# A graph-attention layer whose softmax is one-hot: the last four row blocks reordered, and the unused general path's transfers moved to another queue

## The chip, the cores and the metric

The kernel runs on one core of a Trainium2 chip. The core has five engines with instruction streams of their own: TensorE (PE in the profile; PEld is its weight load), VectorE (DVE), ScalarE (ACT), GpSimd (POOL) and SyncE (SP). Each works through its stream in order, and they meet through semaphores. 16 DMA engines move data between HBM and SBUF. Here SP issues nearly all plain transfers, and POOL the gathers, whose addresses are computed on the chip.

The metric is device time in microseconds (us), the median of several executions. The profile is one further execution, whose span runs from the first instruction to the last. Times such as "at 215.65" are counted from the start of that span.

## The reference, cut to what matters

```python
x: (4096, 512)   adj: (4096, 4096), about 0.4% of it nonzero, values up to 1e9
W: (512, 4*512)  a: (4, 2*512, 1)

ht  = (x @ W).reshape(N, 4, 512).transpose(1, 0, 2)
src = einsum('hnd,hd->hn', ht, a[:, :512, 0])
dst = einsum('hnd,hd->hn', ht, a[:, 512:, 0])
e   = leaky_relu(src[:, :, None] + dst[:, None, :], 0.01) + adj[None]
att = softmax(e, axis=-1)
g   = einsum('hij,hjd->hid', att, ht).mean(axis=0)
y   = x + g
out = (y - mean(y)) / sqrt(var(y) + 1e-5)      # over each row of 512
```

The adjacency values are so large that in nearly every row the largest one leads the next by far more than the attention terms can make up. The softmax is then 1 at that column c and 0 elsewhere, for all four heads, so g = x[c] @ (mean of W over the heads).

## The kernel before, in words

The kernel has two paths. `leading_rows` computes the whole output by the shortcut, and at the same time tests whether every row leads by enough. If a row does not, the flag `any_bad` is positive and `general` computes the exact attention. With these inputs the flag is zero, so `general` (line 529 on) is compiled and never entered. The branch is at line 62: every engine loads the flag (L61) and jumps. A hint placed in the loop tells PE, ACT, DVE and POOL about that branch; SP has no hint.

Rows are taken in 32 blocks of 128, numbered 0 to 31. For one block:

1. SP loads the block of adj, 2 MB (L118). DVE takes the maximum of each segment of 32 columns (L163) and finds the leading segment (`find_segment`, L170 and L172).
2. POOL computes its row number (L174), gathers the segment again from HBM ("lead", L176) and keeps its start (L181).
3. `find_column`: DVE finds the position inside the segment (L198), POOL adds the start (L200) and gathers the 128 rows x[c] ("y", L186).
4. `turn`: PE transposes y (L213), ACT copies the result to SBUF as `yt` (L215). `products`: PE multiplies with the mean weight, four matmuls per block that add up in PSUM ("o", L228). `residual` adds x by one more matmul with the identity (L221).
5. The row statistics are made on ACT (`stats`, L250 and L252) with a small POOL part (`rstd`, L255 to L257), or on DVE with one square root on ACT (`moments`, `factor`). The row is scaled on ACT (`finish`, L261) or on DVE (`normalise`, L297) into `hold`, the SBUF array that held x and now holds the output, and SP stores it (`store`, L313).

The order of the work is written out by hand, and each engine runs it in program order. One step t of the loop works on several blocks at once: it reduces block t, finds the column of block t-2, and turns and multiplies block t-3. The last blocks are treated in their own ways. Blocks 24 to 27 (`BEHIND` to `LATE`-1) are multiplied without x, put by in SBUF (`put_by`, L241), and get x later (`add_x`, L244, three on POOL and one on DVE). Blocks 28 and 29 get x by `residual` matmuls issued in the last step (L442, L443). Block 30 gets it on DVE from PSUM (L511). Block 31 is handled in two halves of columns, each with its own PSUM bank (L266, L270, L304, L309, L310); its column is found in the full row of adj (L206) and needs no segment.

Stores are held back: SP's queue issues its loads first, and the stores of blocks 0 to 23 follow the last loads (L465 to L468). Then come the stores of blocks 28, 29, 24 and 25, 30, 26 and 27, and 31 (L523 to L525). The semaphores of SP's transfers are eight in rotation, so a transfer is not issued before the eighth one before it has landed, and a store whose data is late holds up all later ones. The gathers on POOL have eight semaphores of their own.

Of the kernel before, what the change touches and what calls it, by code (L numbers as in the profile page):

```python
# [20 lines left out]
P = 128  # L21
# [45 lines left out]
def leading_rows(ctx, tc, x, adj, W, a, out, ident, v, n_bad, any_bad):  # L67
# [100 lines left out]
    def find_segment(ib):  # L168
        seg = seg_of.pop(ib)
        nc.vector.max(out=top[:, ib, :], in_=seg)  # L170
        at = small.tile([P, 8], U32, name="at")
        nc.vector.max_index(at, top[:, ib, :], seg)  # L172
        row = small.tile([P, 1], U32, name="row")
        nc.gpsimd.tensor_tensor(row, at[:, 0:1], first[:, ib : ib + 1], op=OP.add)  # L174
        lead = lead_pool.tile([P, E], F32, name="lead")
        nc.gpsimd.indirect_dma_start(  # L176
            out=lead, out_offset=None, in_=adj_segs,
            in_offset=bass.IndirectOffsetOnAxis(ap=row[:, :1], axis=0),
        )
        start = at_of[ib] = small.tile([P, 1], U32, name="start")  # L180
        nc.gpsimd.tensor_tensor(start, at[:, 0:1], width, op=OP.mult)  # L181
        lead_of[ib] = lead

# [78 lines left out]

    def residual_in_halves(ib):
        o_ps[ib] = [psum.tile([P, D // 2], F32, name="o") for _ in range(2)]
        for k, o in enumerate(o_ps[ib]):
            nc.tensor.matmul(o, ident, hold[:, ib, ts(k, D // 2)], start=True, stop=False)  # L266
# [22 lines left out]
    def factor(ib, shift=False):  # L289
        nc.vector.reciprocal(rt[ib], rt[ib])  # L290
        if shift:
            nc.vector.scalar_tensor_tensor(
                nm[:, ib : ib + 1], mean_var[ib][:, 0:1], -1.0, rt[ib], op0=OP.mult, op1=OP.mult
            )
# [111 lines left out]
    COLUMN, PROJECT, STATS, FINISH = 2, 3, 4, 6  # L406

    for t in range(NB):
# [92 lines left out]
    report(pg)  # L501
    turn(NB - 1)
# [14 lines left out]
    finish(BEHIND + 2)  # L517
    finish(BEHIND + 3)
# [4 lines left out]
    for ib, n in ((NB - 4, 1), (NB - 3, 1), (BEHIND, 2), (NB - 2, 1), (BEHIND + 2, 2)):  # L523
        store(nc.sync, ib, n)
# [4 lines left out]
def general(ctx, tc, x, adj, W, out, ident, v, n_bad):  # L529
# [20 lines left out]
    with ExitStack() as pre:  # L550
# [3 lines left out]
        for g in range(NCH):  # L554
            nc.gpsimd.dma_start(x_sb[:, ts(g, Q), :], x_blocks[:, ts(g, Q), :])
        for kb in range(KB):
            nc.gpsimd.dma_start(w_sb[:, kb, :], w_blocks[:, kb, :])
# [29 lines left out]
    def block(ib):  # L587
# [4 lines left out]
        nc.gpsimd.dma_start(adj_t, adj[ds(ib, P, NB), :])  # L592
# [39 lines left out]
        nc.gpsimd.dma_start(r, x[ds(ib, P, NB), :])  # L632
# [10 lines left out]
        nc.gpsimd.dma_start(out[ds(ib, P, NB), :], r)  # L643
# [35 lines left out]
```

## Time and profile before

| what | value |
|---|---|
| median of 3 runs | 235.95 us (235.95 to 236.46) |
| the profiled execution's own time | 236.21 us |
| its span | 234.6 us |
| mean granted clock of TensorE | 0.975 |
| busy: PE, DVE, ACT, POOL | 195.2, 188.4, 111.6, 101.2 us |
| moved by DMA | 97.21 MB, mean 414 GB/s |
| DMA engines busy, from 0 to 202 us / from 207.6 to 229.3 us | 1.00 / 0.97 |
| a 128x512 add on POOL (L244) / on DVE (L244) | 1.28 / 0.67 us |
| a residual matmul, 128x512 (L221) | two passes, 0.43 us each |

The profile is a page of views: the share of time each engine is busy, the span in 40 slices, the queues, the chain of work that ended last, and the groups of instructions. The chain starts at the last instruction of the program and goes back, at each step, to what released it; it ends in the work that set the end. A busy engine that is not in the chain sets nothing. Further views list a stretch in order of time, or one line's instructions with the waits on their queue (marked with a small q, as PEldq).

### The profile page before, as it was taken

To read this page: it belongs to the slowest core of one execution; us is meant where nothing else is said; L and a number is where in the kernel's file an instruction comes from. 1 tells how busy PE (TensorE), PEld (TensorE's weight loads), DVE (VectorE), ACT (ScalarE), POOL (GpSimd) and SP (SyncE) were. 2 spreads that over 40 slices of the span, in tenths; PEclk is the share of its full clock that TensorE was granted. 3 is DMA by queue.
4 is the path that set the end of the run, shared out by engine and by line. 5 is a ranking of instruction groups with operands and counts; after the bars stand their busy time and mean duration, and the time that the engine had idled before them with its cause. 6 is when DMAs were issued, how large, how long until landed. Compare 5 with 4: busy or idle time off the path is not lost.

```text
span 234.6 us, 2498 instructions
## 1 busy us (share of the span) xinstructions
PE 195.2 (83%) x683; PEld 101.4 (43%) x683; DVE 188.4 (80%) x302; ACT 111.6 (48%) x267; POOL 101.2 (43%) x215
## 2 busy tenths in 40 slices
PE   0188929999999999999979879797998968698990
PEld 0034514756565655555534333242443423244460
DVE  1736875589869995999589989998799999989672
ACT  2012011255474747474758354646464645166582
POOL 1012232414527462646353645464365464549130
PEclk9999977999999999999999999999799999999998
DMA  6999999999999999999999999999999999999985
GB/s 226 439 428 426 443 425 430 415 440 412 440 420 426 424 437 434 425 424 428 427 432 433 425 433 422 432 418 429 425 432 418 422 425 427 411 425 419 417 355 210
DMA packets 13697, 97.21 MB, mean 414 GB/s; under 512 B 2152, under 2 KB 2664, under 8 KB 7792
## 3 DMA queue, kind: packets, MB, share of 16 engines
q1 hardware_dynamic: 10080, 88.08, 88.9%
q0 software_dynamic: 3584, 8.92, 9.6%
q8 instruction: 6, 0.10, 0.2%
q14 instruction: 11, 0.09, 0.1%
q10 hardware_dynamic: 16, 0.02, 0.0%
HBM read 88.62 MB, written 8.39 MB: 414 GB/s over the span
## 4 chain that ended last, share of the span: by engine, by line
DMA 45%; POOL 17%; issue 15%; PE 10%; DVE 9%; ACT 1%; POOLq 0%; SPq 0%; DVEq 0%
DMA adj_t<-in_adj_dram 42%; DVE seg L163 8%; PE o L228 7%; POOL lead L176 6%; POOL y L186 5%; DMA y<-in_x_dram,col 3%; POOL sd L256 2%; PE o L270 2%; POOL start L181 1%; POOL row L174 1%; POOL col L200 1%; PE tp L213 1%; PE o L221 1%; ACT yt L215 1%; POOL sd L255 1%
## 5 line engine op out<-in xcount | busy, mean ns | idle before, releaser
L163 DVE TENSOR_REDUCE seg<-adj_t 128x64 f32<-128x2048 f32 (+1 forms) x68 | 146.0, 2149 | 32.7 <-DMA adj_t<-in_adj_dram 32.3
L228 PE MATMUL o<-w_sum,yt 128*128 128x512 f32 x248 | 115.1, 605 | 1.7 <-ACT yt L215 1.7
L228 PEld LDWEIGHTS o<-w_sum,yt 128*128 128x128 f32 x248 | 44.5, 191 | 54.8 <-issue 42.3
L215 ACT COPY yt<-tp 128x512 f32<-128x512 f32 x32 | 18.8, 588 | 44.3 <-PE tp L213 44.3
L176 POOL DMA_INDIRECT lead<-in_adj_dram,row x32 | 32.3, 1010 | 15.5 <-POOL row L174 15.0
L186 POOL DMA_INDIRECT y<-in_x_dram,col x32 | 30.9, 965 | 15.4 <-POOL col L200 15.2
L318 PE MATMUL o<-hold,ident 128*128 128x512 f32 x32 | 18.9, 745 | 17.5 <-DMA hold<-in_L_gnn_W_dram 17.5
L213 PE MATMUL tp<-ident,y 128*128 128x128 f32 x128 | 20.0, 280 | 12.6 <-DMA y<-in_x_dram,col 12.6
L221 PE MATMUL o<-hold,ident 128*128 128x512 f32 x52 | 27.3, 611 | 0.0
L213 PEld LDWEIGHTS tp<-ident,y 128*128 128x128 f32 x128 | 14.9, 143 | 25.4 <-issue 25.0
L174 POOL TENSOR_TENSOR row<-at,first 128x1 uint32<-128x1 uint32 x32 | 6.1, 190 | 42.0 <-DVE at L172 42.0
L336 ACT COPY wt<-tp 128x512 f32<-128x512 f32 x16 | 9.2, 587 | 31.4 <-PE tp L334 31.4
L200 POOL TENSOR_TENSOR col<-start,within 128x1 uint32<-128x1 uint32 x31 | 5.9, 190 | 40.1 <-DVE within L198 40.1
L235 ACT ACTIVATE sq<-hold 128x512 f32<-128x512 f32 x32 | 19.8, 619 | 0.0
L342 PEld LDWEIGHTS pv<-at_d,wt 128*128 128x128 f32 x128 | 16.3, 191 | 6.8 <-ACT wt L336 4.0
L318 PEld LDWEIGHTS o<-hold,ident 128*128 128x128 f32 x32 | 7.4, 243 | 26.7 <-POOL row L174 11.0
L319 ACT ACTIVATE w_sum<-o 128x512 f32<-128x512 f32 x4 | 2.4, 598 | 33.9 <-PE o L318 33.9
L261 ACT ACTIVATE hold<-o,nm,sd 128x512 f32<-128x512 f32 x24 | 17.2, 771 | 0.0
L252 ACT ACTIVATE sq<-o,nm 128x512 f32<-128x512 f32 x24 | 16.5, 688 | 0.8
L342 PE MATMUL pv<-at_d,wt 128*128 128x2 f32 x128 | 15.3, 244 | 0.6 <-ACT wt L336 0.6
L250 ACT ACTIVATE sq<-o 128x512 f32<-128x512 f32 x24 | 14.6, 609 | 0.0
L334 PEld LDWEIGHTS tp<-ident,hold 128*128 128x128 f32 x64 | 7.9, 142 | 6.9 <-issue 6.9
(85 smaller groups left out, 139.8 us busy)
## 6 DMA issues: line engine op xcount, KB each, us to landing
adj_t<-in_adj_dram SPq DMA_DIRECT2D x27, 2048.0 KB, 31.3
hold<-in_x_dram SPq DMA_DIRECT2D x7, 1024.0 KB, 33.2
adj_t<-in_adj_dram SPq DMA_DIRECT2D x6, 1024.0 KB, 25.7
out_dram<-hold SPq DMA_DIRECT2D x10, 512.0 KB, 15.2
adj_t<-in_adj_dram SPq DMA_DIRECT2D x8, 512.0 KB
hold<-in_L_gnn_W_dram SPq DMA_DIRECT2D x4, 1024.0 KB
out_dram<-hold SPq DMA_DIRECT2D x2, 1024.0 KB
hold<-in_x_dram SPq DMA_DIRECT2D x2, 512.0 KB, 14.1
```

Of the source, the lines that this page charges most:

```text
L163: nc.vector.tensor_reduce(seg_of[ib][:, ts(k, S // n)], adj_t[ib][:, ts(k, N // n)].rearrange("p (s e) -> p s e", e=E), axis=AX.X, op=OP.max,)
L176: nc.gpsimd.indirect_dma_start(out=lead, out_offset=None, in_=adj_segs, in_offset=bass.IndirectOffsetOnAxis(ap=row[:, :1], axis=0),)
L186: nc.gpsimd.indirect_dma_start(out=y, out_offset=None, in_=x, in_offset=bass.IndirectOffsetOnAxis(ap=col[:, :1], axis=0),)
L213: nc.tensor.transpose(tp[:, kb, :], y[:, ts(kb, P)], ident)
L215: nc.scalar.copy(yt, tp)
L221: nc.tensor.matmul(o_ps[ib], ident, hold[:, ib, :], start=start, stop=False)
L228: nc.tensor.matmul(o_ps[ib], yt_of[ib][:, kb, :], w_sum[:, kb, :], start=(start and kb == 0), stop=(kb == KB - 1),)
L235: nc.scalar.activation(sq, hold[:, ib, :], AF.Square, accum_out=xx[:, ib : ib + 1])
L252: nc.scalar.activation(sq, o, AF.Square, bias=nm[:, i], accum_out=sd[:, i])
L261: nc.scalar.activation(hold[:, ib, :], o_ps.pop(ib), AF.Identity, bias=nm[:, i], scale=sd[:, i])
L318: nc.tensor.matmul(o, ident, hold[:, w_at + kb * H + h, :], start=(h == 0), stop=(h == H - 1))
L342: nc.tensor.matmul(pv[:, kb, h : 2 * H : H], wt[:, k, :], at_d[:, k, h : 2 * H : H], start=(k == 0), stop=(k == KB - 1),)
```

## The change

The change has five parts.

- **General path.** All plain transfers of `general`, which POOL issued, are issued by SP. The path is still not entered.
- **Late residuals.** The two `residual` matmuls of blocks 28 and 29 are gone. A new `add_residual` adds x on DVE while reading the product from PSUM, as was already done for block 30. In return, `add_x` of block 27 goes from DVE to POOL, and block 28 is finished on ACT and no longer on DVE. Blocks 26 and 27 are finished on POOL (`finish_on_chip`) and no longer on ACT. `turn` of block 29 comes ahead of block 31's two x matmuls.
- **One-input shift.** In `factor`, one `scalar_tensor_tensor` becomes a `tensor_scalar` with the same operands.
- **Gathers.** `find_segment` is split. In the last step, the segment of block 31 is fetched by POOL after the y gather of block 30, and its start is not computed. Only `add_x` of block 24 stands between that fetch and the y gather of block 31; `add_x` of 27, 25 and 26 follow.
- **Stores.** The held stores go out in another order (`HELD`), two-block stores mixed with the two of four blocks, and the last ones are 28, 24 and 25, 26 and 27, 29, 30, 31.

```diff
     def find_segment(ib):
...
-        at = small.tile([P, 8], U32, name="at")
+        at = at_of[ib] = small.tile([P, 8], U32, name="at")
         nc.vector.max_index(at, top[:, ib, :], seg)
+        if ib < NB - 1:
+            fetch_segment(ib)
+
+    def fetch_segment(ib):
+        at = at_of.pop(ib)
         row = small.tile([P, 1], U32, name="row")
         nc.gpsimd.tensor_tensor(row, at[:, 0:1], first[:, ib : ib + 1], op=OP.add)
...
+    def finish_on_chip(ib):
+        i, h = slice(ib, ib + 1), hold[:, ib, :]
+        o_ps.pop(ib)
+        nc.gpsimd.tensor_scalar(h, h, sd[:, i], nm[:, i], op0=OP.mult, op1=OP.add)
+
+    def add_residual(ib):
+        nc.vector.tensor_add(hold[:, ib, :], o_ps[ib], hold[:, ib, :])
+        o_ps[ib] = hold[:, ib, :]
...
-            nc.vector.scalar_tensor_tensor(
-                nm[:, ib : ib + 1], mean_var[ib][:, 0:1], -1.0, rt[ib], op0=OP.mult, op1=OP.mult
+            nc.vector.tensor_scalar(
+                nm[:, ib : ib + 1], mean_var[ib][:, 0:1], rt[ib], -1.0, op0=OP.mult, op1=OP.mult
             )
...
+    HELD = ((8, 2), (10, 2), (0, Q), (12, 2), (14, 2), (Q, Q), (16, 2), (18, 2), (20, 2), (22, 2))
...
-            residual(LATE)
-            residual(LATE + 1)
...
-    for ib in range(0, 2 * Q, Q):
-        store(nc.sync, ib, Q)
-    for ib in range(2 * Q, BEHIND, 2):
-        store(nc.sync, ib, 2)
+    for ib, n in HELD:
+        store(nc.sync, ib, n)
     find_column(NB - 2)
+    fetch_segment(NB - 1)
     add_x(nc.gpsimd, BEHIND)
-    add_x(nc.gpsimd, BEHIND + 1)
     find_column_in_row(NB - 1)
-    add_x(nc.gpsimd, BEHIND + 2)
+    for ib in (LATE - 1, BEHIND + 1, BEHIND + 2):
+        add_x(nc.gpsimd, ib)
     products(LATE, KB - 1, KB)
+    turn(NB - 3)
     residual_in_halves(NB - 1)
-    turn(NB - 3)
     products(NB - 3, 0, KB - 1)
+    bound(0)
+    stats(BEHIND)
+    add_residual(LATE)
     moments(LATE)
+    bound(1)
+    factor(LATE, shift=True)
     for ib in range(BEHIND, NB):
         find_inner(ib)
-    bound(0)
     products(NB - 3, KB - 1, KB)
-    stats(BEHIND)
-    factor(LATE)
-    normalise(LATE, o_ps.pop(LATE))
-    bound(1)
     turn(NB - 2)
+    finish(LATE)
+    moments(LATE - 1)
+    stats(BEHIND + 1)
     bound(2)
-    add_x(nc.vector, LATE - 1)
-    stats(BEHIND + 1)
-    moments(LATE - 1)
-    products(NB - 2, 0, 2)
     bound(3)
     test()
+    products(NB - 2, 0, KB - 1)
     pg = count()
-    products(NB - 2, 2, KB - 1)
     stats(BEHIND + 2)
     rstd(slice(BEHIND, BEHIND + 2))
     rstd(slice(BEHIND + 2, BEHIND + 3))
+    add_residual(NB - 3)
+    turn(NB - 1)
     moments(NB - 3)
     report(pg)
-    turn(NB - 1)
     factor(LATE - 1, shift=True)
     factor(NB - 3)
     normalise(NB - 3, o_ps.pop(NB - 3))
     finish(BEHIND)
     finish(BEHIND + 1)
+    finish_on_chip(BEHIND + 2)
+    finish_on_chip(BEHIND + 3)
     products(NB - 2, KB - 1, KB)
     products_of_half(NB - 1, 0)
     products_of_half(NB - 1, 1)
-    nc.vector.tensor_add(hold[:, NB - 2, :], o_ps[NB - 2], hold[:, NB - 2, :])
-    o_ps[NB - 2] = hold[:, NB - 2, :]
+    add_residual(NB - 2)
     moments(NB - 2)
     stats_of_half(NB - 1, 0)
     factor(NB - 2)
     normalise(NB - 2, o_ps.pop(NB - 2))
-    finish(BEHIND + 2)
-    finish(BEHIND + 3)
...
-    for ib, n in ((NB - 4, 1), (NB - 3, 1), (BEHIND, 2), (NB - 2, 1), (BEHIND + 2, 2)):
+    for ib, n in ((LATE, 1), (BEHIND, 2), (BEHIND + 2, 2), (NB - 3, 1), (NB - 2, 1)):
         store(nc.sync, ib, n)
...
-            nc.gpsimd.dma_start(x_sb[:, ts(g, Q), :], x_blocks[:, ts(g, Q), :])
+            nc.sync.dma_start(x_sb[:, ts(g, Q), :], x_blocks[:, ts(g, Q), :])
...
-        nc.gpsimd.dma_start(adj_t, adj[ds(ib, P, NB), :])
+        nc.sync.dma_start(adj_t, adj[ds(ib, P, NB), :])
...
```

The other three transfers of `general` (the weights, x of a block and the store) change in the same way.

More of the change, by code (lines that the diff above doesn't have):

```diff
@@ L179, in find_segment @@
         )
-        start = at_of[ib] = small.tile([P, 1], U32, name="start")
-        nc.gpsimd.tensor_tensor(start, at[:, 0:1], width, op=OP.mult)
         lead_of[ib] = lead
+        if ib < NB - 1:
+            start = at_of[ib] = small.tile([P, 1], U32, name="start")
+            nc.gpsimd.tensor_tensor(start, at[:, 0:1], width, op=OP.mult)
     def gather_rows(ib, col):
@@ L554, in general @@
         for g in range(NCH):
-            nc.gpsimd.dma_start(x_sb[:, ts(g, Q), :], x_blocks[:, ts(g, Q), :])
+            nc.sync.dma_start(x_sb[:, ts(g, Q), :], x_blocks[:, ts(g, Q), :])
         for kb in range(KB):
-            nc.gpsimd.dma_start(w_sb[:, kb, :], w_blocks[:, kb, :])
+            nc.sync.dma_start(w_sb[:, kb, :], w_blocks[:, kb, :])
         for g in range(NCH):
@@ L631, in block @@
         r = turned.tile([P, D], F32, name="y_g")
-        nc.gpsimd.dma_start(r, x[ds(ib, P, NB), :])
+        nc.sync.dma_start(r, x[ds(ib, P, NB), :])
         nc.vector.tensor_add(r, r, held)
@@ L642, in block @@
         nc.vector.tensor_scalar(r, r, mv[:, 0:1], sd, op0=OP.subtract, op1=OP.mult)
-        nc.gpsimd.dma_start(out[ds(ib, P, NB), :], r)
+        nc.sync.dma_start(out[ds(ib, P, NB), :], r)
     with tc.For_i(0, NB, 1) as ib:
```

## The prediction, on record before the run

> **What bounds the kernel now.** I read the page first: the 40 slices, then the chain that ended last.
>
> ```profile
> DMA  6999999999999999999999999999999999999985
> ...
> DMA 45%; POOL 17%; issue 15%; PE 10%; DVE 9%; ACT 1%; POOLq 0%; SPq 0%; DVEq 0%
> ```
>
> The DMA engines are full up to slice 38, so until about 223 us bytes set the pace, and no part of the change removes a byte. Only the tail can be shortened. The chain in order of time shows it:
>
> ```profile
> 196.17 7.27 DMA y<-in_x_dram,col
> ...
> 204.21 3.57 PE o L228 x8
> 207.78 1.72 PE o L221 x4
> ...
> 224.40 0.44 PE tp L213 x4
> 224.83 0.86 PE o L228 x2
> 225.69 3.55 PE o L270 x16
> 229.27 0.44 DVE halves_st L304
> ...
> 230.69 0.56 ACT hold L310
> ```
>
> From 203.6 to 229.3 PE works nearly without a gap; then the last block's statistics, its scaling, its store at 231.29 (SP's stream) and 2.3 us to landing. The two residual matmuls are in this chain: 1.72 us. What could stop PE from starting sooner are the y gathers. TensorE's queue reads ahead, so the time at which it passes the wait for a gather is the time at which the gather landed. L213's view in four narrow windows gives 207.6, 213.0, 218.5 and 222.8 for blocks 28 to 31; the second and fourth:
>
> ```profile
> L213 PEldq EVENT_SEMAPHORE  x1: 51/51/51, 213.0 to 213.0; - x1
> ...
> L213 PEldq EVENT_SEMAPHORE  x1: 51/51/51, 222.8 to 222.8; - x1
> ```
>
> PE transposed these blocks at 209.33, 215.01, 219.93 and 224.23: slacks of 1.8, 2.0, 1.4 and 1.5 us. So 1.72 us less on PE brings two gathers to the edge. POOL's timeline says when they are issued:
>
> ```profile
> 211.54 0.19 POOL L200 TENSOR_TENSOR col<-start,within 128x1 uint32<-128x1 uint32 x1
> 212.00 0.97 POOL L186 DMA_INDIRECT y<-in_x_dram,col  x1 [0.27 <-POOL col L200]
> 212.99 2.50 POOL L244 TENSOR_TENSOR hold<-hold,adj_t 128x512 f32<-128x512 f32 x2
> 215.65 0.96 POOL L186 DMA_INDIRECT y<-in_x_dram,col  x1 [0.16 <-PE tp L213]
> ```
>
> Last, both ends of the program, from the views of L665 (the entry) and L674 (the exit):
>
> ```profile
> L665 POOLq MOVE  x4: 29/29/35, 0.2 to 0.4; - x4
> ```
>
> ```profile
> L674 SPq EVENT_SEMAPHORE  x14: 17/28/28, 232.8 to 234.5; - x14
> ```
>
> SP's twelve closing waits run from 232.84 to 233.62, some 0.063 apart; the last one is for the last store, and 0.94 us of barrier follows.
>
> **What the Trainium skill says.** "DMA: Bandwidth & Descriptors", section "SWDGE vs HWDGE vs iDMA": POOL's gathers and SP's transfers feed different queues in each DMA engine, which takes them in turn. The trace agrees: a store of 512 KB took 15.2 us to land behind others, while these four y gathers took 6.05, 6.97, 6.48 and 7.12 us from POOL's issue to PE. So the new order of stores should hardly move the gathers, though they scatter by 0.5 us either way. "Runtime: NRT & Kernel Launch", section "Instruction fetch mechanics": a taken branch whose target is outside the fetched pages stalls. In the trace SP's branch costs nothing visible (0.05 us, next wait 0.18 us later).
>
> **The change part by part**, in the clock of the profile before.
>
> *Start.* In the built program the four register moves that POOL made for its transfers before the first barrier (0.21 to 0.42, 0.06 apart) are SP's now. POOL reaches the barrier last, SP idles there. All starts 0.24 us sooner: -0.24 (bounds -0.3 and 0).
>
> *PE up to block 30.* Turning 28 follows at 207.61 where the residuals stood (its gather: 207.55): -1.72. Five matmuls later PE is free at 214.14 - 1.72 = 212.42, but block 29's gather, which is not moved, lands at 213.02: PE idles 0.6 us. That gap costs little: the two x matmuls of block 31 (0.86 us) now stand behind the turn and cover ACT's copy, which before left PE idle (1.27 us from turn to product). Products of 29 start at 213.13 + 0.44 + 0.86 = 214.43, before at 216.28: -1.85. Turning 30 then falls at 219.93 - 1.85 = 218.08. Its gather: `within` ends at 210.34, POOL answers 0.09 later, 0.70 from the add to the gather as at 209.71, so 211.13 and not 212.00; landing 218.48 - 0.87 = 217.6. It is in time.
>
> *Block 31's gather.* POOL: gather of 30 until 212.10, row 0.2, lead from 212.82 to 213.79, one add of 1.28 to 215.1, then 0.16: issued at 215.26 (DVE's index is ready at 214.84), before 215.65. Landing 222.77 - 0.39 = 222.38. PE would be free at 222.10 (219.36 for the products of 30, three of 0.86, the count 0.15). So the gather decides: turn 31 at 222.48, before 224.23: -1.75. Everything PE does after it keeps that; its end is 227.52.
>
> *DVE.* It gains two adds from PSUM (0.69 as at L511), loses one `add_x` (0.67) and one scaling from PSUM (0.81); scaling 29 from SBUF takes 0.55 as for block 30. In order: after L206 (214.84) `xm`, add 28, its moments to 216.6, `xg` at 217.42 (after PE), two small ones, eight maxima of 0.09. The last needs block 31's lead, issued 2.4 us later than before: landing 215.75 + 2.42 = 218.2, needed at 218.6. Moments of 27 to 219.7, the test to 220.9 (before 222.3), add and moments of 29 to 222.4, report to 222.8, scaling of 29 at 224.1 (it waits for ACT's root behind `yt` of 31), add of 30 at 224.65, and by the distances before (2.89) scaling of 30 ends near 227.4. PE ends at 227.52: hidden, by 0.1 us only.
>
> *ACT.* `yt` of 30 at 218.72, finish 28 (0.8), root, stats of 25 and 26 (1.5 each) to 223.1; `yt` of 31 wanted at 223.12. Hidden, again with nothing over.
>
> *POOL and SP.* rstd of 26 ends at 224.3, then two `tensor_scalar` of 512 elements, which no row shows: below, 0.19 us (a small one, L255); above, the two-input add, 1.28. "GPSIMD Engine Reference", sections 3.1 and 4.1: one-input operations are roughly line-rate, about 1 cycle per element for up to two operations, 1.8 for a plain loop. At its 1.2 GHz that is an estimate of 0.45 to 0.77 us, plus 0.19: I take 0.8, range 0.19 to 1.28. Store of 26 and 27 at 226.0, ahead of 29, 30 and 31 on SP. The held stores drain until about 226; 1.5 MB (24 to 27, 29, 30) at 410 GB/s end near 230, when store 31, issued at 231.29 - 1.75 = 229.54, begins to move. Hidden up to 1.3 us per operation.
>
> *One-input shift.* 0.16 us either way: 0 (bounds ±0.05).
>
> *End.* This one costs. `general` now uses SP's semaphores, so in the built program the untaken side has SP wait for all eight of them and raise them. The eighth wait is for store 31. Only after it come the twelve closing waits, which before ran while the store was landing: 233.62 - 232.84 = 0.78. The eight new waits themselves hide: before, SP stood at its closing waits 1.55 us after it issued store 31, eight more at 0.063 make 2.05, and the landing takes 2.3. All other engines then wait for SP at the barrier. +0.78; bounds 0.5 (closing waits already met might pass faster) and 1.0 (one more jump).
>
> Sum: -0.24 - 1.75 + 0.78 = -1.21. Against the profiled execution: 236.21 - 1.21 = 235.0. That execution lies 0.26 above the median, so 235.95 - 1.21 = **234.75 us**.
>
> **Rivals.**
>
> *Gathers take the place of the residuals.* PE then only waits longer. For it: all four slacks are 1.4 to 2.0 us, and the gathers scatter. Against: two gathers are issued sooner. If block 31's takes 7.5 to 7.8 us and lands at 222.8 to 223.1, the tail gains 1.35 to 1.05: 235.15 to 235.45. A shorter one gains nothing more, since ACT and DVE have nothing over.
>
> *No gain: the stores set the end.* The DMA engines stay full to 226 whatever PE does. If the drain is 1 us longer or the mixed packets slower, store 31 queues, and about 235.9 results. Against: 0.74 busy after 226.
>
> *SP's branch.* SP's skipped code grows from 45 to 82 instructions in the built program. If the target is then no longer fetched, a stall stands before the closing waits. No view shows what one costs; 0.3 us of it is hidden, 0.8 would take the gain below 0.7, and 1.5 would end at 235.95. Against: before, the jump was free.
>
> *Slower: POOL's scaling holds up SP.* If one `tensor_scalar` takes T, store 26-27 goes out at 224.4 + 2T; it and three more stores need about 4.6 us to land (1.28 MB at 410 GB/s, 1.5 of latency). Later than now, 233.6 - 0.54, from T = 2.0; at T = 2.5 the landing is at 234.0 and the time 235.95 + 0.4 + 0.54 = 236.9. For it: two operations in one instruction are unknown here. Against: an add with two inputs takes 1.28.
>
> **How the numbers follow.** The forecast 0.56 (234.3 to 235.15), gathers 0.17, stores 0.09, SP's branch 0.08, POOL 0.10. A measurement of this kernel tells about 0.3% from no change, 0.7 us: faster means below 235.24. Forecast and part of the gathers: 0.62. Same: rest of the gathers, stores, branch: 0.28. Slower: POOL, 0.10. The range 234.2 to 236.0 leaves POOL and some edges out.
>
> **What would show it.** Right: no L221 after 207 us; PE idle near 213 for 0.6 us before block 29's turn; block 31's turn near 222.2 (0.24 sooner in all); SP's closing waits all behind the last landing. Wrong: POOL's two operations above 1.3 us, a DVE wait for lead near 218, PE waiting past 222.8 for block 31, or a pause of SP after its branch.

## The result, and the profile after

The changed kernel takes 236.91 us (median of 16 executions, 236.24 to 238.29) against 236.23 us for the kernel before (16 executions, 235.63 to 237.01): a ratio of 1.0038, with a 95% interval of 1.0024 to 1.0052. It is slower by 0.7 us. The forecast was 234.75 us. Executions in a slower state (two in e1, one in e10, two in e12, one in e17) are left out of all medians and ratios below.

The profiled execution took 236.44 us, with the same span as before, 234.6 us. The page looks much the same too: the DMA engines are full for as many slices, and the chain that ended last has less PE (8% and not 10%) and more POOL and issue.

```profile
DMA  6999999999999999999999999999999999999985
...
DMA 36%; issue 23%; POOL 23%; PE 8%; DVE 6%; ACT 1%; SPq 1%; POOLq 0%; DVEq 0%
```

The chain in order of time (start, length, what) answers to the one shown of before:

```profile
201.43 7.39 DMA y<-in_x_dram,col
208.96 0.63 PE tp L219 x4
209.59 4.38 PE o L234 x10
...
224.44 3.58 PE o L285 x16
228.04 0.44 DVE halves_st L319
...
229.53 0.56 ACT hold L325
```

The two residual matmuls are gone, and TensorE ends at 228.00, 1.23 us sooner than the 229.23 of before. The forecast was 1.71 in the clock of before, so 1.95 with the 0.24 us by which everything was to start sooner. The first row shows where it was lost: block 28's gather, issued at 201.43 (before: 201.50), took 7.4 us and not 6.05. TensorE now waits for it, where before it had 1.8 us in hand. This is L219 (the transposes) in the window from 208 to 210:

```profile
L219 PEldq EVENT_SEMAPHORE  x1: 51/51/51, 208.9 to 208.9; - x1
...
  DMA y<-in_x_dram,col: 2.5, 1
```

Blocks 28 to 31 are transposed at 208.96, 213.80, 218.72 and 222.92 (before: 209.33, 215.01, 219.93, 224.23). The gather of block 31 was passed at 222.31, so it was not what held its turn.

POOL's timeline shows the moved gathers, nearly where they were foreseen. Block 31's was to be issued at 215.26 and went out at 215.93, though the start was 0.24 us sooner:

```profile
211.54 0.97 POOL L192 DMA_INDIRECT y<-in_x_dram,col  x1 [0.60 <-POOL col L206]
...
213.00 0.97 POOL L181 DMA_INDIRECT lead<-in_adj_dram,row  x1 [0.27 <-issue]
213.99 1.28 POOL L250 TENSOR_TENSOR hold<-hold,adj_t 128x512 f32<-128x512 f32 x1
215.93 0.97 POOL L192 DMA_INDIRECT y<-in_x_dram,col  x1 [0.66 <-issue]
```

The last stores are L328 on SP's queue. The row gives the shortest, median and longest issue in ns, and below it the time from issue to landing:

```profile
L328 SPq DMA_DIRECT2D out_dram<-hold x5: 332/383/1044, 225.9 to 230.1; - x5
...
DMA to landing us min/median/max: 2.8/2.8/2.8
```

The same view of the kernel before:

```profile
L313 SPq DMA_DIRECT2D out_dram<-hold x5: 332/332/333, 225.5 to 231.3; - x5
...
DMA to landing us min/median/max: 2.3/2.3/2.3
```

Block 31's store goes out at 230.12, 1.17 us sooner than before, but lands 2.8 us later and not 2.3. One issue, that of blocks 26 and 27, took 1.04 us. Then the exit (L62 is the untaken branch's join, L686 the closing waits):

```profile
L62 SPq EVENT_SEMAPHORE  x9: 17/17/17, 231.9 to 232.9; - x9
```

```profile
L686 SPq EVENT_SEMAPHORE  x14: 17/28/28, 232.9 to 234.5; - x14
```

Of the nine waits at L62 the last is for the last landing: SP passes it at 232.88. Then come the twelve closing waits, up to 233.62. In the kernel before, SP passed the same landing at 233.62 as its last closing wait. So in this pair of profiles the landing is 0.74 us sooner, and the closing waits behind it take 0.74 us: the barrier begins at the same time. (0.24 of these 0.74 us is the earlier start of the program.)

A second profile of the unchanged changed kernel (e12 below) took 236.88 us and had a span of 235.0 us. It has block 28 late again (transposed at 209.19), TensorE's end at 228.37, an issue of 1.08 us, and a landing 2.85 us after the issue at 230.48.

### The profile page after: what moved, and what is told of

It is laid out like the page before. It is cut to its first block, busy times and chain, and to the rows that moved or that the text cites. A ratio compares the mean times of both kernels' runs of the same rounds, so it can differ in the third digit from the quotient of the medians.

```text
span 234.6 us, 2493 instructions
## 1 busy us (share of the span) xinstructions
PE 193.9 (83%) x679; PEld 100.5 (43%) x679; DVE 188.0 (80%) x303; ACT 111.1 (47%) x266; POOL 103.9 (44%) x217
## 4 chain that ended last, share of the span: by engine, by line
DMA 36%; issue 23%; POOL 23%; PE 8%; DVE 6%; ACT 1%; SPq 1%; POOLq 0%; DVEq 0%
DMA adj_t<-in_adj_dram 30%; POOL lead L181 8%; POOL y L192 7%; PE o L234 5%; DVE seg L163 5%; DMA y<-in_x_dram,col 3%; DMA lead<-in_adj_dram,row 3%; POOL sd L262 3%; POOL row L179 2%; POOL start L188 2%; PE o L285 2%; POOL col L206 1%; PE tp L219 1%; POOL sd L261 1%; SPq L118 1%
## 5 line engine op out<-in xcount | busy, mean ns | idle before, releaser
L234 PEld LDWEIGHTS o<-w_sum,yt 128*128 128x128 f32 x248 | 45.3, 194 | 55.8 <-issue 43.9
L333 PE MATMUL o<-hold,ident 128*128 128x512 f32 x32 | 17.9, 710 | 17.5 <-DMA hold<-in_L_gnn_W_dram 17.5
L219 PE MATMUL tp<-ident,y 128*128 128x128 f32 x128 | 19.7, 277 | 12.6 <-DMA y<-in_x_dram,col 12.5
L227 PE MATMUL o<-hold,ident 128*128 128x512 f32 x48 | 26.2, 629 | 0.0
L219 PEld LDWEIGHTS tp<-ident,y 128*128 128x128 f32 x128 | 14.5, 141 | 25.3 <-issue 24.3
L333 PEld LDWEIGHTS o<-hold,ident 128*128 128x128 f32 x32 | 6.9, 226 | 26.2 <-POOL row L179 10.7
```

What stands on the lines that cost most here:

```text
L219: nc.tensor.transpose(tp[:, kb, :], y[:, ts(kb, P)], ident)
L227: nc.tensor.matmul(o_ps[ib], ident, hold[:, ib, :], start=start, stop=False)
L234: nc.tensor.matmul(o_ps[ib], yt_of[ib][:, kb, :], w_sum[:, kb, :], start=(start and kb == 0), stop=(kb == KB - 1),)
L333: nc.tensor.matmul(o, ident, hold[:, w_at + kb * H + h, :], start=(h == 0), stop=(h == H - 1))
```

## The experiments

Each kernel ran in five rounds beside the kernel before, on one chip. Ratios are to the kernel before, with 95% intervals; they need not be the quotient of the medians.

### The place of the general path alone (e2), and the tail alone (e1)

e2 is the kernel before with only this edit, at all five transfers of `general`; e1 is the changed kernel with the same edit the other way.

```diff
-            nc.gpsimd.dma_start(x_sb[:, ts(g, Q), :], x_blocks[:, ts(g, Q), :])
+            nc.sync.dma_start(x_sb[:, ts(g, Q), :], x_blocks[:, ts(g, Q), :])
```

> The kernel before with only the general path's transfers moved to SP. Theory: +0.74 for the closing waits, -0.24 for the start, so 0.5 us more than before, ratio about 1.0021, with the last store's landing at the same distance from its issue. Rival (free, or only the start counts): ratio 0.999 to 1.000.

> The changed kernel with the general path's transfers back on POOL; all else as changed. Theory (SP's new waits stand behind the last landing, and POOL's four moves open the program): the first load 0.24 us later, the twelve closing waits again under the landing of store 31, 0.74 us less: 0.5 us less than the changed kernel, ratio to before about 1.0017. Rival (this part costs nothing, all of the loss lies in the reordered tail): as the changed kernel, about 1.0038.

e2: 237.12 us, ratio 1.0029 (1.0014 to 1.0043). Code that is never entered costs 0.7 us by its place. In its profile SP passes the wait for the last landing at 233.66 and ends its closing waits at 234.40; before, one time did for both, 233.62.

e1: 236.91 us, ratio 1.0026 (1.0005 to 1.0047). The closing waits are back under the landing, and still nothing is gained. In its profile TensorE ended at 229.33, no sooner than before, and the last landing was passed at 234.00, later than the 233.62 of before. Last of all ended a chain of which the prediction knew nothing, L686 on POOL's queue:

```profile
L686 POOLq DRAIN  x3: 40/103/5306, 229.3 to 235.2; - x3
```

After POOL has joined, it drains for 5.3 us, here from 229.32 to 234.63; SP was ready at 234.12. With the general path on POOL a further instruction (INC_SWDGE_SEM, 1.48 us) stands ahead of the drain, and the two scalings of blocks 26 and 27 come ahead of that. In the kernel before the drain ended at 233.54, just under the last landing. With the general path on SP there is no INC_SWDGE_SEM; in the changed kernel the drain starts at 226.14, ends at 231.95, and hides. (It takes 5.8 us there, as in the seven other profiles in which the two scalings are still running when it starts, and 5.3 us in all others.)

### TensorE's work put back (e3), and the gathers out of its way (e4)

e3 puts two matmuls on TensorE where the residuals stood, into the bank that block 28's products then overwrite. e4 makes TensorE transpose something that is there:

```diff
         if t == NB - 1:
...
+            o_ps[LATE] = psum.tile([P, D], F32, name="o")
+            for late in (LATE, LATE + 1):
+                nc.tensor.matmul(o_ps[LATE], ident, hold[:, late, :], start=True, stop=True)
```

```diff
         y = y_t.pop(ib)
+        if ib >= LATE:
+            y = hold[:, 0, :]
```

> The changed kernel with two 128x512 matmuls of the identity put back on PE where the residuals stood; their result is overwritten and used for nothing. Theory (the gather of block 28 gates PE, which idled 2.5 us there in the changed kernel's profile): the 1.72 us fit into the idle time, the time stays within 0.4 us of the changed kernel, ratio about 1.004. Rival (PE work sets the tail): 1.7 us more, ratio about 1.011.

> The changed kernel, but blocks 28 to 31 transpose a finished block from SBUF and not their gathered rows, so that PE never waits for these four gathers; the gathers still run, and the outputs of these four blocks are left wrong. Theory (waits for gathers eat the saving): block 28's turn near 207.3, PE ends 1.5 to 1.9 us sooner, then the queue of the last stores takes over; 0.5 to 1.2 us less than the changed kernel, ratio 0.999 to 1.002. Rival (gathers do not matter): ratio about 1.0038.

e3: 236.60 us, ratio 1.0018 (1.0001 to 1.0035); e4: 236.72 us, ratio 1.0014 (1.0002 to 1.0025). The matmuls can come back at no loss, and taking away TensorE's waits for the last four y gathers brings the end no nearer than 0.1% above the kernel before. But e4 did not give the shorter tail that was expected of it: TensorE ended at 228.15, no sooner than in the changed kernel (228.00). It started block 31 at 222.06, and then waited for ScalarE. VectorE had waited for the segment of block 31, which the change fetches later and this edit leaves as it is; behind that came ScalarE's statistics of blocks 25 and 26, and then its copy of block 31:

```profile
219.65 0.19 DVE L198 MAX8 inner<-lead 128x8 f32<-128x32 f32 x1 [1.01 <-DMA lead<-in_adj_dram,row]
...
224.43 3.72 PE L287 MATMUL o<-w_sum,yt 128*128 128x256 f32 x16 [0.85 <-ACT yt L223]
```

Block 31's store was issued at 230.26 and landed 3.2 us later. So TensorE's removed work does not set this kernel's end, and the y gathers alone do not either.

### The order of the held stores (e7, e8), SP's hint (e6), and the changed kernel again (e12)

e7 is the kernel before with the new `HELD` order, e8 the changed kernel with the old one:

```diff
-    for ib, n in HELD:
-        store(nc.sync, ib, n)
+    for ib in range(0, 2 * Q, Q):
+        store(nc.sync, ib, Q)
+    for ib in range(2 * Q, BEHIND, 2):
+        store(nc.sync, ib, 2)
```

e6 adds SP to the engines that are told of the branch:

```diff
-HINTED = tuple(getattr(mybir.EngineType, name) for name in ("PE", "Activation", "DVE", "Pool"))
+HINTED = tuple(getattr(mybir.EngineType, name) for name in ("PE", "Activation", "DVE", "Pool", "SP"))
```

> The kernel before with only the new order of the held stores. Theory (the order of these stores moves no byte and hardly moves the gathers): no difference, ratio 0.999 to 1.001. Rival (the new order delays the gathers of blocks 28 and 29, which landed 1.3 us later in every changed kernel than in the profile of the kernel before): block 28's gather lands near 208.8 and not 207.5, ratio 1.002 to 1.004.

> The changed kernel with the held stores in their old order. Theory (the order does nothing): within 0.1% of the changed kernel, ratio to the kernel before 1.003 to 1.004. Rival (the new order costs the tail, by a later gather of block 28 or by a worse end of the stores): 0.5 to 1.0 us less than the changed kernel, ratio 0.999 to 1.001, block 28's gather landing near 207.5 and TensorE ending near 226.8.

> The changed kernel with SyncE added to the engines that the hint in the loop tells of the branch. Theory (the jump over the longer skipped code costs SyncE a fetch of about 0.3 us, but the wait for the last store's landing covers it): SyncE goes from its branch to the first wait in 0.2 us and not in 0.5, the last closing wait does not move, and the time stays within 0.1% of the changed kernel. Rival (the stall is on the path): 0.3 us less, ratio to the kernel before 1.001 to 1.002 with the changed kernel at 1.003 to 1.004.

> The changed kernel as it is, beside the others on one chip, for a second profile. Theory: ratio 1.003 to 1.004 again; block 28's gather lands at 208 to 209, with 0.5 us of scatter from profile to profile; one of SyncE's last stores again takes over 1 us to issue, and the last landing takes over 2.6 us. Rival (the late gather and the slow issue were chance in one profile): block 28 at 207.5 and all stores at 0.33 us.

e7: 236.37 us, 0.9996 (0.9979 to 1.0012): the order of the held stores does nothing. e8: 237.15 us, 1.0026 (1.0004 to 1.0048), not told from the changed kernel. e12: 236.98 us, 1.0033 (1.0017 to 1.0049), as the first time. e6: 237.47 us, 1.0046 (1.0025 to 1.0067). Here the expectation failed at its first step: from branch to first wait SP still takes 0.52 us. It takes 0.50 to 0.52 in all eleven profiles with the general path on SP and 0.18 in all nine with it on POOL, so the jump over the longer skipped code takes 0.3 us more, and the hint doesn't prevent it. Whether it would cost anything stays untested; in the changed kernel SP, having passed the other waits at 232.42, stood 0.46 us at the last one, so there it is covered. In e2 and e9 SP went through all nine waits without a pause, so there little or nothing is left over.

e8 had block 28's gather on time and block 29's late instead: it landed at 214.47. That pointed to the cause of the late gathers. In all 20 profiles TensorE's instruction queue (q8) moves one packet of 16 KB between 201 and 218 us; it takes some 0.95 us, and the gather that is under way at that time is the late one. These are the rows of the DMA view that tell where the packet falls, the changed kernel from 205 to 209:

```profile
q0 software_dynamic: 103, 0.28, 18.1%
q8 instruction: 1, 0.02, 1.5%
```

and e8 from 210 to 214:

```profile
q0 software_dynamic: 80, 0.26, 16.6%
q8 instruction: 1, 0.02, 1.5%
```

From issue to its last packet, block 28's gather takes 6.6 to 6.9 us in the ten profiles with that packet in its way, and 5.4 to 5.7 us in the other ten. Block 29's takes 7.5 us in e6, e8 and e11, where the packet falls on it (6.9 in e15, where it comes near the end), and 6.2 to 6.6 us without. In the profile of before it fell on block 27's gather, in that of e2 on block 28's. It comes with TensorE's 599th to 640th matmul in the records, not at the same one in every build. It was not moved on purpose, so this is a match in 20 profiles and not a test.

### GpSimd free early (e5, e11), and the same tail with the general path on SP (e9)

e5 is e1 with blocks 26 and 27 finished on ScalarE as before, and the last stores in the old order. e11 also takes the last three small operations from POOL. e9 is e5 with the general path on SP.

```diff
-    finish_on_chip(BEHIND + 2)
-    finish_on_chip(BEHIND + 3)
...
     normalise(NB - 2, o_ps.pop(NB - 2))
+    finish(BEHIND + 2)
+    finish(BEHIND + 3)
```

```diff
-    rstd(slice(BEHIND + 2, BEHIND + 3))
...
     finish(BEHIND + 1)
+    c = slice(BEHIND + 2, BEHIND + 3)
+    nc.scalar.activation(sd[:, c], sd[:, c], AF.Sqrt, bias=eps, scale=1.0 / D)
...
     moments(NB - 2)
+    nc.vector.reciprocal(sd[:, c], sd[:, c])
     stats_of_half(NB - 1, 0)
+    nc.scalar.activation(nm[:, c], nm[:, c], AF.Identity, scale=sd[:, c])
```

> The changed kernel with the general path's transfers on GpSimd again (so no closing waits behind the last landing), and with blocks 26 and 27 finished on ScalarE at their old place and the last stores in their old order, so that GpSimd reaches the branch about 1.8 us sooner. Theory (the changed tail saves 1.0 to 1.2 us on TensorE, but with the general path on GpSimd the drain of GpSimd, 5.3 us after its last instruction, ended last): the drain ends by 233.7, under the last landing, and the time falls to about 235.6, ratio 0.997 or less, 1.1 us below the run with the general path on GpSimd alone. Rival (the tail's gain is lost in the queue of stores, wherever the closing work stands): 236.4 to 237.0, ratio 1.000 to 1.003, the last landing taking 2.8 us or more.

> The run with the general path on GpSimd and blocks 26 and 27 finished on ScalarE, with one more edit: the last three small operations of GpSimd (rstd of block 26) become a square root and a product on ScalarE and a reciprocal on VectorE, so that GpSimd reaches its branch some 1.0 us sooner. Theory (GpSimd's final drain, about 8 us from its last operation to its end, ended last there, at 233.4, after the last landing at 233.0): the drain ends near 232.4, the span shrinks by 0.3 to 0.4 us, time about 235.8, ratio 0.997 to 0.998. Rival (the drain only waits for something that ends late anyway): it still ends at 233.4 and the time is that of the earlier run, ratio 0.999.

> The changed kernel, general path on SyncE as changed, but blocks 26 and 27 finished on ScalarE at their old place and the last stores in their old order. It parts the two costs: against the run with the same tail and the general path on GpSimd (ratio 0.999) only the end of the program differs. Theory (closing waits behind the last landing cost 0.7 us on SyncE, and the tail's order of stores costs the rest): SyncE issues none of the last stores in more than 0.5 us; last landing 2.3 to 2.5 us after issue, near 232.8; time 0.3 to 0.5 us above the kernel before, ratio 1.001 to 1.002, so below the changed kernel. Rival (only the place of the general path matters): ratio 1.003 to 1.004, as the changed kernel.

e5: 236.18 us, 0.9992 (0.9969 to 1.0015), where 0.997 or less was foreseen. It is the best of these tails, and no better than the kernel before. In its profile (235.75 us) the last landing was passed at 232.98, and the drain ended last, at 233.4. e11: 236.37 us, 1.0014 (0.9999 to 1.0028). Its drain ended at 232.91 and no longer mattered, but the landing, at 233.68, did, and the time did not fall: the drain is one limit of several. e9: 236.80 us, 1.0038 (1.0016 to 1.0061), against 0.9992 for the same tail with the general path on POOL. That is what the rival said, but the two did not run on one chip, and e9's profile has TensorE at half its clock from 209.5 to 212.9; e16 below is the cleaner test.

### Both kernels without the gathers (e13, e14), and the price of the closing waits (e16)

e13 is e11, e14 the kernel before, each with the edit of e4; e16 is e13 with the general path on SP.

> The run that freed GpSimd early (general path on GpSimd), with TensorE transposing block 0 of hold in place of the gathered rows of blocks 28 to 31; the gathers still run, the outputs of these four blocks are not those of the reference. Theory (late gathers eat the tail's gain): TensorE ends near 228.1, last landing near 232.6, no closing waits behind it; time 235.2 to 235.7, ratio 0.996 to 0.998, runs within 1.5 us of each other. Rival (something else at the end holds the time): 236.2 or more, ratio 0.999 or above.

> The kernel before with the same edit (blocks 28 to 31 transpose block 0 of hold; outputs of these four are not those of the reference). Theory (its slack at each gather covered the late ones): nothing gained, ratio 0.999 to 1.001, TensorE ends at 229.2 to 229.8 as before. Rival (gathers held the kernel before too): TensorE ends 0.5 us or more sooner, ratio 0.998 or less.

> The first of these four kernels with the general path's transfers on SyncE; nothing else differs. Theory (the closing waits stand behind the last landing): 0.6 to 0.8 us more than that kernel, ratio 0.999 to 1.001, the twelve closing waits taking 0.74 us after the last landing. Rival (the waits are of no weight once the gathers are out): within 0.2 us of that kernel.

e14: 236.31 us, 0.9991 (0.9974 to 1.0008), as foreseen in the time, but not in TensorE's end, 228.05. The 16 KB packet fell on block 28's gather here, for which TensorE no longer waited; block 27's, passed at 203.47 in the profile of before, was passed at 202.29, and the queue behind it moved up. Where the packet falls on block 28's gather and TensorE does wait, as in e2, it stands idle, and ends at 229.25:

```profile
209.32 0.63 PE L213 MATMUL tp<-ident,y 128*128 128x128 f32 x4 [0.78 <-DMA y<-in_x_dram,col]
```

So late gathers cost TensorE some 1.2 us in the kernel before too, and its time does not change without them. e16 against e13, on one chip and differing in nothing else: 236.95 against 236.30 us, 1.0023 (1.0005 to 1.0040) against 0.9998 (0.9983 to 1.0013). That is 0.65 us for the general path on SP, with 0.74 us of closing waits behind the landing in the profile.

e13 is the run that decides about the tail, and it went against the theory that the gathers eat the gain. TensorE ended at 227.20, 2.0 us sooner than in the kernel before, and block 31's store was issued at 229.32, 2.0 us sooner. The time did not move. The DMA view from 229 to 234 (40 slices of 0.125 us, and the stores issued in it) shows where the 2 us went:

```profile
DMA  9999999999999994755623211010010100000000
...
out_dram<-hold SPq DMA_DIRECT2D x1, 256.0 KB, 4.4
```

The same view of the kernel before:

```profile
DMA  3122899989999799997111001898994110000000
...
out_dram<-hold SPq DMA_DIRECT2D x1, 256.0 KB, 2.3
```

In the kernel before, the queue is nearly empty from 231.4 to 232.0, and block 31's store passes in one burst. In e13 the store goes in behind others, and after 231.5 a thin trickle goes on to 233.3: a DMA share of 0.08 from 232 to 233, about one engine of 16. The landing takes 4.4 us. e14 shows the same in the old order: issued at 230.10, landed 3.8 us later.

### What makes the last landing late (e10, e15, e17, e18)

e10 leaves the store of blocks 26 and 27 out of the changed kernel; e17 leaves those of 24 to 27 out of e13, e18 out of the kernel before. e15 is the changed kernel with the last stores in the old order.

```diff
-    for ib, n in ((LATE, 1), (BEHIND, 2), (BEHIND + 2, 2), (NB - 3, 1), (NB - 2, 1)):
+    for ib, n in ((LATE, 1), (BEHIND, 2), (NB - 3, 1), (NB - 2, 1)):
```

The same line in e17 and e18 (where it has NB - 4 for LATE, the same block), and in e15:

```diff
+    for ib, n in ((LATE, 1), (NB - 3, 1), (NB - 2, 1)):
```

```diff
+    for ib, n in ((LATE, 1), (NB - 3, 1), (BEHIND, 2), (NB - 2, 1), (BEHIND + 2, 2)):
```

> The changed kernel without the store of blocks 26 and 27, so that rows of these two blocks are missing from the output; all of their computation stays. Theory (the last 1.75 MB of stores, issued after 225.8, fill SyncE's queue until 231.5, and block 31's store lands late behind them): block 31's store lands 2.0 to 2.2 us after its issue and not 2.8, so the time falls by 0.6 us against the changed kernel. Rival (the last landing is latency alone): the landing still takes 2.7 us or more and the time stays within 0.2 us of the changed kernel.

> The early tail without gather waits (general path on GpSimd) without the two stores of blocks 24 to 27; their rows are missing from the output, and the outputs of blocks 28 to 31 are not those of the reference. Theory (1.75 MB of late stores in one queue, slowest DMA engine last, hold the last landing at 233 to 234 however early block 31 is ready): with 0.75 MB in it, block 31's store, issued near 229.3, lands 2.2 to 2.6 us later, near 231.7; time 234.3 to 234.9, ratio 0.991 to 0.995. Rival (the landing is late for another reason): still 233 or later, ratio 0.998 or above.

> The kernel before without the two stores of blocks 24 to 27, whose rows are missing from the output. Theory (in the kernel before, block 31 is ready so late that the queue has run dry by then): block 31's store still lands 2.2 to 2.4 us after its issue near 231.3, nothing is gained, ratio 0.998 to 1.001. Rival (bytes set its end too): 0.5 us or more less, ratio 0.998 or less.

> The changed kernel with the last stores in the order of before: 28, 29, 24 and 25, 30, 26 and 27, 31; blocks 26 and 27 still finished on GpSimd. Theory (a store that SyncE issues while TensorE's next instructions are being fetched, 1.0 to 1.5 us from about 226.2 on, takes over 1 us to issue): no store is issued in that stretch, all of the last stores take 0.4 us or less; time within 0.3 us of the changed kernel, ratio 1.001 to 1.004. Rival (the store of 26 and 27 is slow because GpSimd has just written its data): it takes 1 us at its new place too.

The theory of the full queue explains at most a small part. e17: 236.20 us, 0.9980 (0.9964 to 0.9997), the lowest ratio of all but with rows missing, where 0.995 or less was foreseen; block 31's store went into an empty queue and landed 3.1 us after its issue. Its profile, at 236.98 us, is the longest of those counted, with TensorE at half its clock from 205.2 to 208.6, so the store went out at 231.12 and not near 229.3. e10: 238.11 us, 1.0061 (1.0034 to 1.0089), landing 3.0 us after issue; why it is 1.1 us slower than e12 beside it is not known (in its profile TensorE is at half its clock from 209.4 to 212.8). e18: 237.43 us, 1.0040 (1.0028 to 1.0053), landing 2.9 us after issue, and 0.9 us slower than the kernel before though it stores 1 MB less. In e18's profile the whole stream is late from far ahead of the missing stores (the first held store goes out at 200.09, against 199.08 to 199.76 in before and e7), so it says little of the end; why is not known. Fewer bytes in the queue did not shorten the time from issue to landing in any of the three.

What makes it long is only argued. Each engine ends its share of a transfer with a packet of 4 bytes. For block 31's store the median engine writes it 1.5 to 1.6 us after the issue in 19 of the 20 profiles (2.2 in e13), whatever stands in the queue. It is the last engine that differs. It comes after the median by

```
e2 0.14  e7 0.16  before 0.17  e11 0.25  e9 0.37   e5 0.48   e15 0.50  e8 0.54  changed 0.56  e1 0.61
e3 0.64  e6 0.64  e12 0.65     e18 0.77  e10 0.90  e4 1.03   e17 1.12  e14 1.15  e16 1.39  e13 1.68
```

us, and the wait is passed another 0.4 to 1.1 us later. So one or two of the 16 engines come in late. The three longest belong to the stores that go out first (e13, e16, e14), but e10 and e18, whose stores go out last (at 232.0), are late as well, so the time of the issue alone does not set it.

Instruction packets are in the way at these times (q8, 16 KB, 1.0 to 1.6 us when TensorE jumps; q14, 8 KB, 0.3 to 0.8 us, at the other engines' jumps). The records don't name the engine of a packet, but the times hint at it: in e1, e4, e10, e13, e14, e16, e17 and e18 a packet of SP's queue starts 3 or 4 ns before a q14 packet ends, as the next one on the same engine would. These are all seven profiles whose last engine is more than 0.7 us late, and e1; in the other twelve there is no such pair. In the kernel before, the first of the last jumps comes at 232.98, 1.7 us after the store's issue and behind its data.

The instruction packet is not all of it. In e14 the last engine still moves a 4 KB packet of an earlier store at 231.71, when the median engine is done with block 31's, so it was behind already; in e4, e13, e16, e17 and e18 some 2 KB packets behind the instruction packet take 0.12 to 0.29 us and not 0.08. This is a match in the profiles; no run moved the jumps, so the cause of the late engine stays open.

e15, L328 on SP's queue:

```profile
L328 SPq DMA_DIRECT2D out_dram<-hold x5: 332/333/383, 226.3 to 231.2; - x5
```

No issue is slow, as foreseen. In the profiles of all eight kernels with an issue of 1.0 us or more (after, e1, e3, e4, e6, e8, e10, e12), the slow one starts while TensorE's 16 KB packet is on its way. In the other twelve an issue starts there only in the packet's last 0.2 us (before, e2, e13, e14, e18), and takes 0.33 to 0.56; one issue in e4 stands against it, at 226.78, in 0.33 us. With e15, its place in time is the likelier reason than GpSimd's writing. It costs nothing that shows: 237.32 us, 1.0033 (1.0013 to 1.0053).

## Why the prediction was wrong

**The step that failed** is the tail's term, -1.75, on its way to the last landing, in the paragraph on POOL and SP: "store 31, issued at 231.29 - 1.75 = 229.54, begins to move. Hidden". The sum took TensorE's 1.75 us through to the last landing in full, with 2.3 us from issue to landing, a figure from one profile. Two things took it away. The store was issued at 230.12 and 230.48 in the two profiles of the changed kernel, and not at 229.30 (229.54, less the earlier start), mainly since block 28's gather came late. And the landing took 2.8 us in both. With the 0.24 us of the start taken off, the landing was passed 0.50 us sooner than before in one profile and 0.05 us in the other. The late gathers alone do not explain it: with no waits for them, and 2.0 us saved on TensorE, e13 measures 0.9998 (0.9983 to 1.0013), and the landing takes 3.6 to 4.4 us in e16, e14 and e13. It gives back what TensorE saves. Why it does is not known. In the sum, -1.75 becomes about 0, -0.24 becomes 0 (see the next paragraph), and the +0.78 is left: 236.23 + 0.7 = 236.9, which is what was measured. (The base of 235.95, from three executions, was itself 0.28 us below the 236.23 of sixteen.)

**Start, -0.24.** In the span it is there: the first load goes out at 0.74 and not at 0.98. But the metric doesn't have it. The device time is longer than the span by 1.80 to 1.85 us (means over the executions) in all eleven kernels with the general path on SP, and by 1.57 to 1.62 us in the kernel before and the eight others with it on POOL. What the span gains at its start comes back outside it, where no profile looks; why is not known. So this term was worth nothing. e2 shows the same: its mean span grew by 0.39 us and the time outside it by 0.25, and the 0.54 us that the two terms give became 0.7.

**TensorE, -1.75.** The residuals' time did fall out, but most of it was lost again in waits: TensorE ended 1.23 us sooner and, in the second profile, 0.86 us, with 0.24 us of earlier start in both. In e8, e15 and e6, which differ from the changed kernel in nothing that TensorE does, it was 0.42, 0.14 and 0.10 us. The forecast had block 28 transposed at 207.61 since its gather landed at 207.55 in the profile of before. It landed at 208.85. One landing from one profile stood for a quantity with two values 1.3 us apart. Nor did the kernel before always have the slack of 1.4 to 2.0 us that was read from that profile: in e2 the late gather is block 28's, and TensorE waits for it. As for the rival that gathers take the place of the residuals, block 31's turn at 222.92 falls into the window it named, yet e13 shows that they were not the last limit.

**ScalarE and VectorE, "with nothing over".** Right, and even a little less than nothing: in e4, with the y gathers out of the way, ScalarE's copy of block 31 held TensorE for 0.85 us. The segment of block 31, expected at 218.2 and needed at 218.6, came late there: VectorE waited for it 1.01 us in e4 and 0.51 us in e13, the sign of being wrong that the prediction had named.

**GpSimd's scaling.** Taken at 0.8 us from the price that the Trainium skill gives ("GPSIMD Engine Reference", sections 3.1 and 4.1); the trace has it:

```profile
L272 POOL TENSOR_SCALAR hold<-hold,sd,nm x2: 763/786/808, 225.1 to 225.9; 128x512 f32<-128x512 f32 x2
```

So the rival for a slower kernel, which needed 2.0 us, was wrong. But GpSimd's last work matters in another way, through its drain, as e1 shows; the prediction had no term for that.

**One-input shift, 0.** Not tested alone. In the profiles the new form takes 0.21 us and the old one 0.16 (block 31's, L307 and L292), so it was no gain.

**End, +0.78.** Right: 0.74 in the profile. The place of the general path as a whole cost 0.7 us in e2 and 0.65 us between e16 and e13. Its sign decided the result. All 11 ratios with the general path on SP, the changed kernel's two among them, lie at 1.0014 or above; of the eight with it on POOL five lie below 1, and e11, e1 and e18 at 1.0014, 1.0026 and 1.0040.

**SP's branch.** The Trainium skill ("Runtime: NRT & Kernel Launch", section "Instruction fetch mechanics") lets one fear a stall for a jump beyond what is fetched. SP did take 0.3 us longer after its branch, covered in the changed kernel by the wait for the landing; that a fetch was the reason is not shown.

**Stores set the end.** This rival was the right one in its result, that nothing comes of a shorter tail, and had been given 0.09. Its reason, bytes in the queue, explains at most a small part, as e17 shows. And it was taken as an alternative to the forecast's sum, with 235.9, where the closing waits had to be added on top.

No version with a whole output beat the kernel before. The closest is e5, at 0.9992 (0.9969 to 1.0015).

## What to carry to other kernels

Before you price a shorter tail, list every chain that ends at the barrier and when: here the last landing (233.62) and GpSimd's drain (233.54) stood within 0.1 us of each other, and the time from a store's issue to its landing was not a constant that moves along with the issue. Ask of transfers in a branch that is never taken which engine must wait for whose semaphores where the paths join; here this alone cost 0.7 us, in e2. Compare the span with the measured time too: 0.24 us gained inside the span was not gained at all. And slack at a gather is not idle time to be collected if the gather's latency has two values; take it from several profiles.

## What the runs showed of the hardware

- Instruction packets stand in the DMA records beside the data. TensorE's 16 KB packet takes 0.9 to 1.6 us, and a gather under way at that time finishes 1.0 to 1.3 us later (a match in 20 profiles, not a test). The Trainium skill ("Runtime: NRT & Kernel Launch", section "Instruction fetch mechanics") gives the same block of 16 KB and calls the cost of crossing it mostly hidden; for TensorE itself it is (in e2 it works on without a gap from 206.36 to 207.32, while the packet moves), for the gather under way it isn't.
- GpSimd's drain at the end takes 5.3 us in every profile, and 5.8 us where two scalings of 0.8 us are still running when it starts, so its last operation has to end 5 to 8 us before the barrier.
- A store of 0.25 or 0.5 MB that SP issues while TensorE's 16 KB packet near 227 us is under way takes 1.0 to 1.5 us to issue and not 0.33 (eight profiles, with one issue of 0.33 us against it).
- One engine of 16 can end its share of a 256 KB store 1.7 us after the median one (e13). In all seven profiles where it was more than 0.7 us late, an 8 KB instruction packet seems to stand directly ahead of a packet of a store, which starts 3 or 4 ns before its recorded end.
